# The experts' biases as one float32r product over 128 rows

## The chip, the core and the metric

The kernel runs on one core of a Trainium2 chip. The metric is device time in microseconds (us), the median over runs of the whole program. A profile is one execution recorded by the hardware profiler; its busy times and waits belong to that execution. The engines are named as in the profile: PE is the matrix engine (PEld its weight loads), DVE the vector engine, ACT the scalar engine, POOL the GpSimd engine, and SP the engine that here only issues transfers. Each takes its instructions in program order, and waits on semaphores for the others.

## The reference, cut to what matters

Four residual stages follow each other on 2048 tokens of width 256: cross attention, a mixture of eight experts, a windowed attention over a context of 1601 rows, and a slot layer. The change touches the second:

```python
logits  = einsum('bsd,ed->bse', layernorm(x), router_w) + router_b
probs   = softmax(logits)
weights = max(probs);  top1 = argmax(probs)
y_all   = einsum('bsd,eod->bseo', layernorm(x), expert_w) + expert_b   # 8 experts
y       = take_along_axis(y_all, top1)        # the chosen expert's row
x       = x + y * weights
```

The kernel computes all eight products for each token and weights them with a gate: a row of eight numbers, zero except for the chosen expert, where it holds the weight. The biases then come in as `gate @ expert_b`, a product of a tokens x 8 matrix with an 8 x 256 matrix.

## The kernel before

**Stages.** The attention (lines 720 to 909) takes the first 800 us. Everything after it stands in one part of the program (from line 912), with new pools in the memory that the attention leaves, so its loads cannot start before the attention is over. First come 13 loads on SP's queue (lines 929 to 945: the context, `W_aT`, `W_cT`, the slot layer's weights, about 5 MB) and 13 small ones on POOL's queue (lines 946 to 965). SP's loads are given out over eight semaphores in turn; a load whose semaphore still belongs to an earlier transfer waits, in SP's order, until that one has landed.

**Blocks.** The tokens are cut into five blocks (`BLOCKS`, line 967): three of four tiles of 128 tokens, and two of two tiles. `experts(lb)` (line 1031) walks one block: for every tile, four pairs of experts, each an fp32 product into a PSUM buffer `y_ps` (four of these exist, pool `ps_y`), followed by two DVE instructions that multiply with the gate and add to `x_sb` (line 1048). A `yield` ends each pair. After each second tile the biases are added: two fp32 matmuls with the turned gate as weights, `gT` (8 x 128), and the biases `eb` (8 x 256) as the moving side (line 1059), and one DVE addition (line 1061).

**The turned gate.** `turned_gate` (line 1010) runs once per block, after the first tile: it transposes the gate, 128 x 8 per tile, into a PSUM bank (pool `ps`, three banks, function `bank`) and copies it on ACT to `gT`, 8 x 512. `eb` was loaded with the experts' weights (line 144), at 203 us in the profile.

**What runs beside.** Between two pairs, `aside(3)` (line 1391) advances up to three other generators by one step each: `front` of the next block (layer norm, transposes, routing), `window` (a preparation for the third stage, once), `slots` (a preparation for the fourth, once), and, for blocks already through the experts, `windowed` followed by `weights`. The order of these steps is the program order of each engine; the scheduling of this part is by hand. When the blocks are through, the remaining generators run alone, with filler matmuls (`busy`), and the slot layer ends the program.

**Names for the steps of the prediction.** Line 107 is the normalizing DVE instruction of the layer norm, line 102 its POOL instruction (`ln_rstd`), line 1001 the transposes that wait for it; lines 1072 to 1136 are DVE's part of `window`; line 1115 its first instruction in the second step. Line 1233 is the ACT tanh into `th` and line 1235 the POOL addition that reads it; `th` has two buffers. Line 1312 is a large POOL addition in `weights`, line 1351 the DVE product `alpha`. Line 1369 is a subtraction on 64 partitions that makes a second part of a float32r number, and line 1523 a float32r product of 128 rows by 256 columns in the slot layer's end.

## Time and profile before

| | us |
|---|---|
| median of three runs (1083.15, 1085.77, 1083.15) | 1083.15 |
| the profiled execution | 1085.9 |
| its span | 1084.1 |
| PE busy, matmuls | 961.7 (89%) |
| DVE busy | 749.3 (69%) |
| ACT busy | 516.9 (48%) |
| POOL busy | 71.9 (7%) |
| last attention matmul ends, loads of the second part start | 800.5 |
| block 0 of the experts, first and last pair | 800.4 to 859 |
| last expert pair of the last block | about 1013 |

The profile's page gives busy time by engine, then the span in 40 slices, then the queues, then the chain of work that ended last, followed back from the last instruction to what released each step, then the costliest groups of instructions. Further views answer questions on one engine in one stretch: its instructions in order of time, with the idle time before each and what ended it. An fp32 matmul stands in the records as two instructions, a float32r matmul as one. Busy shares are averages over stages with different limits; for a change in one stage, what counts is which engine is waited for there.

### The profile page before, as it was taken

What the parts mean: (1) busy time and instruction counts of PE and PEld (TensorE: products, weight loads), DVE (VectorE), ACT (ScalarE), POOL (GpSimd) and SP (SyncE); (2) the same over time, 40 slices, a digit from 0 to 9 for tenths busy, and PEclk for the clock granted to TensorE, in tenths of its full rate; (3) what the DMA queues carried; (4) which work ended last, traced back from release to release, by engine and by line L of the source; (5) the groups of instructions that cost most, each with busy time, mean ns of one, the idle gap of its engine ahead of it and who ended that gap; (6) DMA issues with size and microseconds to landing.
All of it is one profiled execution on the core that took longest, in us unless ns stands there. A gap on an engine that the chain in (4) does not pass through costs nothing.

```text
span 1084.1 us, 14756 instructions
## 1 busy us (share of the span) xinstructions
PE 961.7 (89%) x5742; PEld 448.1 (41%) x5742; DVE 749.3 (69%) x1415; ACT 516.9 (48%) x614; POOL 71.9 (7%) x96
## 2 busy tenths in 40 slices
PE   6787888989989899898889989899997999999986
PEld 2234333444443343343334434344343455545543
DVE  6456867878777787878787876977016566675754
ACT  2423546666646565656566665665840011221331
POOL 4000200000010000001000000000020003021210
PEclk8777979999999999999999999998998999999999
DMA  4763721310102100001210110100033000000002
GB/s 157 162 150 93 145 71 44 107 27 3 28 2 71 60 13 28 16 13 28 88 29 2 28 28 2 28 2 1 2 108 116 1 1 0 1 1 1 1 0 78
DMA packets 32277, 46.96 MB, mean 43 GB/s; under 512 B 6412, under 2 KB 21269, under 8 KB 31951
## 3 DMA queue, kind: packets, MB, share of 16 engines
q1 hardware_dynamic: 30478, 43.65, 15.0%
q10 hardware_dynamic: 1232, 1.61, 0.4%
q8 instruction: 45, 0.74, 0.3%
q0 software_dynamic: 496, 0.76, 0.3%
q14 instruction: 26, 0.21, 0.1%
HBM read 26.77 MB, written 14.04 MB: 38 GB/s over the span
## 4 chain that ended last, share of the span: by engine, by line
PE 67%; DVE 24%; issue 4%; DMA 2%; ACT 1%; POOL 1%; SPq 0%; POOLq 0%; DVEq 0%; ACTq 0%
PE acc L849 18%; PE s_ps L883 14%; DVE mx L262 12%; PE a_ps L257 11%; PE y_ps L1041 7%; PE a_ps L240 2%; DVE xn L107 2%; DVE x_sb L1048 2%; PE a_ps L498 1%; PE a_ps L824 1%; PE o_ps L1227 1%; DVE ln_stats L96 1%; PE a_ps L284 1%; PE x_ps L461 1%; PE a_ps L461 1%
## 5 line engine op out<-in xcount | busy, mean ns | idle before, releaser
L262 DVE TENSOR_REDUCE mx<-a_ps 128x2 f32<-128x804 f32 (+1 forms) x645 | 494.2, 799 | 133.9 <-PE a_ps L257 123.4
L888 ACT ACTIVATE es<-s_ps 128x1024 f32<-128x1024 f32 (+1 forms) x416 | 405.6, 1021 | 231.8 <-PE s_ps L883 225.0
L257 PE MATMUL a_ps<-kb,qb 50*128 50x402 bf16 x992 | 235.3, 353 | 47.7 <-DVE mx L262 32.5
L883 PE MATMUL s_ps<-qt,kt 52*128 52x512 f32 (+1 forms) x832 | 242.4, 530 | 2.1 <-DMA qt<-nT 2.1
L849 PE MATMUL acc<-es,v 128*32 128x512 f32 (+1 forms) x1664 | 233.0, 632 | 0.0
L257 PEld LDWEIGHTS <-qb 50*128 50x128 bf16 x1024 | 81.2, 95 | 294.6 <-issue 276.3
L883 PE MATMUL s_ps<-ql,kt 52*128 52x512 f32 (+1 forms) x832 | 196.9, 403 | 0.0
L883 PEld LDWEIGHTS s_ps<-qt,kt 52*128 52x128 f32 (+1 forms) x832 | 102.9, 196 | 29.2 <-ACT es L888 16.1
L883 PEld LDWEIGHTS s_ps<-ql,kt 52*128 52x128 f32 (+1 forms) x832 | 108.5, 192 | 0.4
L1041 PE MATMUL y_ps<-expert_wT_sb,xT 128*128 128x512 f32 x192 | 89.8, 598 | 0.0
L102 POOL TENSOR_TENSOR ln_rstd<-ln_ve,mhalf 128x2 f32<-128x2 f32 (+2 forms) x28 | 21.1, 754 | 781.3 <-DVE ln_ve L100 780.0
L1048 DVE SCALAR_TENSOR_TENSOR x_sb<-y_ps,r_gate,x_sb 128x256 f32<-128x256 f32 x96 | 46.3, 482 | 32.5 <-PE y_ps L1041 30.7
L849 PEld LDWEIGHTS acc<-es,v 128*32 128x32 f32 (+1 forms) x1664 | 33.4, 109 | 54.5 <-issue 52.9
L1041 PEld LDWEIGHTS y_ps<-expert_wT_sb,xT 128*128 128x128 f32 x192 | 34.1, 191 | 31.9 <-issue 30.8
L1004 ACT COPY xT<-tr_ps 128x512 f32<-128x512 f32 (+1 forms) x28 | 13.4, 493 | 53.3 <-PE tr_ps L1001 53.3
L798 DVE RECIPROCAL rec<-a_ps 128x16 f32<-128x16 f32 x16 | 4.1, 258 | 49.4 <-PE a_ps L240 49.4
L107 DVE TENSOR_SCALAR xn<-x_sb,ln_mv,ln_rstd 128x256 f32<-128x256 f32 x64 | 32.8, 554 | 1.1 <-POOL ln_rstd L102 1.1
L1041 PE MATMUL y_ps<-expert_wT_sb,xnT 128*128 128x512 f32 x64 | 32.2, 631 | 0.0
L1001 PE MATMUL tr_ps<-ident,xn 128*128 128x128 f32 x88 | 17.6, 296 | 10.9 <-DVE xn L107 10.9
L284 PE MATMUL a_ps<-ident,nsp 128*8 128x128 f32 x64 | 10.0, 279 | 19.3 <-DVE nsp L275 18.9
L96 DVE BATCH_NORM_STATS2 ln_stats<-x_sb 128x6 f32<-128x256 f32 x64 | 23.3, 413 | 3.4 <-POOL x_sb L1235 3.4
L1048 DVE SCALAR_TENSOR_TENSOR x_sb<-y_ps,gate,x_sb 128x256 f32<-128x256 f32 x32 | 15.4, 483 | 13.6 <-PE y_ps L1041 13.0
(343 smaller groups left out, 727.9 us busy)
## 6 DMA issues: line engine op xcount, KB each, us to landing
qt<-q_rows SPq DMA_DIRECT2D x32, 192.0 KB
q_rows<-qhi SPq DMA_DIRECT2D x8, 512.0 KB
qb<-q_rows SPq DMA_DIRECT2D x30, 96.0 KB
kt<-expert_wT_sb SPq DMA_DIRECT2D x24, 100.5 KB
q_rows<-qp SPq DMA_DIRECT2D x8, 256.0 KB
q_rows<-qlo SPq DMA_DIRECT2D x8, 256.0 KB
ql<-q_rows SPq DMA_DIRECT2D x32, 64.0 KB
expert_wT_sb<-in_expert_wT SPq DMA_DIRECT2D x1, 2048.0 KB
```

Of the source, the lines that this page charges most:

```text
L96: nc.vector.bn_stats(stats[:rows, i, :], src[:, i, :])
L102: nc.gpsimd.tensor_tensor(rstd[:rows, :n], ve[:rows, :n], mhalf[:rows, :n], ALU.pow)
L107: nc.vector.tensor_scalar(dst[:, i, :], src[:, i, :], mv[:rows, i, 0:1], rstd[:rows, i : i + 1], ALU.subtract, ALU.mult,)
L240: nc.tensor.transpose(ps[:, t * P : (t + 1) * P], src[:, t, c * P : c * P + n], ident)
L257: nc.tensor.matmul(ps[:, k, :CH], qb[u % 2][rows, pl, t * P : (t + 1) * P], kb[g][rows, pl, c * CH : (c + 1) * CH], start=True, stop=True,)
L262: nc.vector.tensor_reduce(flat[:, n : self.n], ps[:, : self.n - n, :CH], AX.X, ALU.max)
L461: nc.tensor.matmul(ps[:n, :D], ctxT[:, c, i * P : i * P + n], wv[:, c, :], start=c == 0, stop=c == 1,)
L849: nc.tensor.matmul(acc[HP * j : HP * (j + 1), :], v[:n, i, h * VW : h * VW + HP], es[j // 2][:n, j % 2, :], start=i == 0, stop=i == NS - 1,)
L883: nc.tensor.matmul(ps[:n, h, :], kt[u % NG][rows, pl, i * P : i * P + n], q[u % nq][rows, pl, :], start=k == 0, stop=k == 1,)
L888: nc.scalar.activation(e[:n], ps[:n], AF.Exp)
L1041: nc.tensor.matmul(ps.rearrange("p e d -> p (e d)"), xT[:, c, tok], ew[:, c, pair * 2 * D : (pair + 1) * 2 * D], start=c == 0, stop=c == 1,)
L1048: nc.vector.scalar_tensor_tensor(xb[:, t, :], ps[:, k, :], gate[:, t, e : e + 1], xb[:, t, :], ALU.mult, ALU.add,)
```

## The change

The product with the biases gets 128 rows, in float32r, in place of 8 rows in fp32. The gate is repeated sixteen times side by side (128 x 128 per tile), so that its transpose has the gate in every group of eight rows. Of the transposed gate, rows 0 to 63 keep the first part (the value rounded to float32r) and rows 64 to 127 the second (what the rounding left). The bias tile is zero but for rows 0-7, 32-39, 64-71 and 96-103, which hold the biases; of these, groups 0 and 64 keep the first part and groups 32 and 96 the second. One product over 128 rows then sums all four combinations of parts.

- `bias_parts`, new, is a generator that runs beside block 0. Its first step clears the tile `eb4` on POOL and issues four loads of the biases on SP's queue; its second makes the parts on DVE, with one copy and two subtractions. The load of `eb` at line 144, and the tile, are gone.
- `turned_gate` becomes a generator of three steps, advanced after each of the first pairs of a block's first tile: a POOL copy that repeats the gate (128 x 512 for four tiles), the transposes and the ACT copy (now 128 partitions), and a DVE subtraction on the upper 64 partitions that reads the PSUM bank again.
- `th` has one buffer in place of two.

```diff
-    eb = keep.tile([NE, D], F32, name="eb")
...
-        nc.sync.dma_start(eb, a["expert_b"])
...
+    def bias_parts():
+        eb4 = moe.tile([P, 2, D], F32, name="o", bufs=3)[:, 0, :]
+        nc.gpsimd.memset(eb4, 0.0)
+        for k in range(4):
+            nc.sync.dma_start(eb4[k * 32 : k * 32 + NE, :], a["expert_b"])
+        yield
+        parts = late.tile([P, D], F32R, name="eb_parts")
+        nc.vector.tensor_copy(parts, eb4)
+        for k in (1, 3):
+            rows = slice(k * 32, (k + 1) * 32)
+            nc.vector.tensor_tensor(
+                parts[rows], eb4[rows], parts[rows].bitcast(F32), ALU.subtract
+            )
+        eb_of["parts"] = parts
+        yield
 
     def turned_gate(lb):
         gate, nt = gate_of[lb], BLOCKS[lb][1]
-        ps = bank([NE, nt * P], "g_ps")
+        g16 = moe.tile([P, TPB, P // NE, NE], F32, name="g16", bufs=1)[:, :nt]
+        nc.gpsimd.tensor_copy(g16, gate.unsqueeze(2).to_broadcast([P, nt, P // NE, NE]))
+        yield
+        ps = bank([P, nt * P], "g_ps")
         for t in range(nt):
-            nc.tensor.transpose(ps[:, t * P : (t + 1) * P], gate[:, t, :], ident)
-        gT = moe.tile([NE, LB], F32, name="gT")
+            nc.tensor.transpose(
+                ps[:, t * P : (t + 1) * P], g16[:, t].rearrange("p k e -> p (k e)"), ident
+            )
+        gT = gT_of[lb] = moe.tile([P, LB], F32R, name="gT")
         nc.scalar.copy(gT[:, : nt * P], ps)
-        return gT
+        yield
+        nc.vector.tensor_tensor(
+            gT[NSLOT:, : nt * P], ps[NSLOT:], gT[NSLOT:, : nt * P].bitcast(F32), ALU.subtract
+        )
+        yield
...
+        gT = turned_gate(lb)
         for t in range(nt):
...
+                if t == 0:
+                    next(gT, None)
                 yield
-            if t == 0:
-                gT = turned_gate(lb)
             if t % 2:
...
-                    nc.tensor.matmul(ps[:, k, :], gT[:, tok], eb, start=True, stop=True)
+                    nc.tensor.matmul(
+                        ps[:, k, :], gT_of[lb][:, tok], eb_of["parts"], start=True, stop=True
+                    )
...
-            th = moe.tile([P, 2, D], F32, name="th")
+            th = moe.tile([P, 2, D], F32, name="th", bufs=1)
...
-    beside = [window()]
+    beside = [bias_parts(), window()]
```

In the instruction order that comes of it, SP's four new loads stand behind its 13 loads of the second part, and on four of the eight semaphores: those that last belonged to `w2`, `WhhT`, `WihT` and `wq`. On DVE the three instructions of `bias_parts` stand between the second layer-norm statistics of block 1 (line 100, at 815.9 us in the profile before) and line 1115. On POOL the gate's copy for block 0 stands ahead of the first `ln_rstd`, and the clearing of `eb4` ahead of the index instruction of `window` (line 1086). On PE the transposes for block 0 stand behind the attention's last output product (line 824), and two pairs of `y_ps` that ran ahead of them now follow them.

More of the change, by code (lines that the diff above doesn't have):

```diff
@@ L1005, in normed @@
             yield
-    turned_of, gate_of = {0: xnT}, {0: gate_0}
+    turned_of, gate_of, gT_of = {0: xnT}, {0: gate_0}, {}
+    eb_of = {}
+    def bias_parts():
[13 more added lines that the diff above has]
+        yield
     def turned_gate(lb):
         gate, nt = gate_of[lb], BLOCKS[lb][1]
-        ps = bank([NE, nt * P], "g_ps")
+        g16 = moe.tile([P, TPB, P // NE, NE], F32, name="g16", bufs=1)[:, :nt]
+        nc.gpsimd.tensor_copy(g16, gate.unsqueeze(2).to_broadcast([P, nt, P // NE, NE]))
+        yield
+        ps = bank([P, nt * P], "g_ps")
         for t in range(nt):
-            nc.tensor.transpose(ps[:, t * P : (t + 1) * P], gate[:, t, :], ident)
-        gT = moe.tile([NE, LB], F32, name="gT")
+            nc.tensor.transpose(
+                ps[:, t * P : (t + 1) * P], g16[:, t].rearrange("p k e -> p (k e)"), ident
+            )
+        gT = gT_of[lb] = moe.tile([P, LB], F32R, name="gT")
         nc.scalar.copy(gT[:, : nt * P], ps)
-        return gT
+        yield
[3 more added lines that the diff above has]
+        yield
     def front(lb):
@@ L1034, in experts @@
         xb, nt = of_block(lb)
-        gT = None
+        gT = turned_gate(lb)
         for t in range(nt):
```

## The prediction

> **What bounds the kernel now.** I read the page's chain of waits first, then PE's and DVE's instructions in order of time where the change lies, then SP's, then the table by stretches of time.

> ```profile
> PE 67%; DVE 24%; issue 4%; DMA 2%; ACT 1%; POOL 1%; SPq 0%; POOLq 0%; DVEq 0%; ACTq 0%
> ```

> PE sets the end for two thirds of the span, DVE for a quarter. The change lies behind 800 us. There the table by stretches (columns: stretch, length, busy PE, PEld, DVE, ACT, POOL with counts, granted clock, DMA share, GB/s) says where PE is full:

> ```profile
> 824.00:860.00 36.00, 36.00 (x121) 17.35 (x121) 15.75 (x42) 1.49 (x4) 0.00 (x0) 0.94 0.00 1
> 860.00:911.00 51.00, 49.39 (x184) 27.14 (x183) 33.35 (x104) 6.41 (x12) 6.87 (x9) 1.00 0.00 0
> 911.00:962.00 51.00, 47.74 (x175) 26.41 (x174) 35.81 (x107) 10.11 (x17) 8.35 (x8) 1.00 0.00 1
> 962.00:1004.00 42.00, 38.51 (x152) 22.23 (x151) 30.17 (x93) 10.09 (x19) 7.63 (x7) 1.00 0.00 0
> ```

> From 824 us on PE is busy all the time, then 92 to 97% of it: what PE saves there is saved, and a delay handed to PE at 824 is never made up. Before 824 it is otherwise. PE's lines, then DVE's:

> ```profile
> 814.41 1.88 PE L1041 MATMUL y_ps<-expert_wT_sb,xnT 128*128 128x512 f32 x4
> 820.02 0.65 PE L1001 MATMUL tr_ps<-ident,xn 128*128 128x128 f32 x2 [3.72 <-DVE xn L107]
> 823.33 0.80 PE L1001 MATMUL tr_ps<-ident,xn 128*128 128x128 f32 x2 [2.66 <-DVE xn L107]
> ...
> 815.90 0.17 DVE L100 TENSOR_SCALAR ln_ve<-ln_mv 128x2 f32<-128x2 f32 x1
> 817.08 0.22 DVE L1115 CAST posr<-posr_i 128x64 f32<-128x64 int32 x1 [1.01 <-POOL posr_i L1113]
> ...
> 822.86 0.73 DVE L107 TENSOR_SCALAR xn<-x_sb,ln_mv,ln_rstd 128x256 f32<-128x256 f32 x2
> ```

> PE stands idle for 3.72 and 2.66 us, each time for DVE's normalizing instruction (line 107), and DVE has hardly a gap from 817.08 to 824. So in this stretch DVE's order sets the end, and whatever is put between line 100 and line 1115 goes straight onto the path. The change puts three instructions there, the first of which waits for a transfer.

> **The wait for the biases (the largest term).** The four new loads stand behind SP's big ones. Its last, and the traffic (stretch table, same columns):

> ```profile
> 816.24 2.43 SPq L77 DMA_DIRECT2D wo_sb<-in_wo  x1
> 820.00:822.00 2.00, 0.65 (x2) 0.28 (x2) 1.66 (x11) 0.39 (x2) 0.00 (x0) 0.85 1.12 325
> 822.00:824.00 2.00, 0.68 (x3) 0.53 (x4) 1.95 (x6) 0.29 (x1) 0.00 (x0) 0.50 0.48 154
> ```

> SP is not through with its last issue until 816.24 + 2.43 = 818.67. The third and fourth loads then wait for the semaphores of `WihT` and `wq`. From the sizes, 83% of SP's bytes lie up to `WihT`; summing the GB/s of the 2 us stretches, and taking off POOL's 0.76 MB, they have passed at about 820.5. So the fourth load is issued at about 821.5. The traffic ends at about 823. I let the biases land at 823.5 to 824, say 823.8; ends: 822.7 (with the last big bytes) and 826 (if the four issues take 1 to 3 us as `wo`'s 2.43 did).

> [...]

> What DVE loses: from 817.08 to 823.8 is 6.7 us. The copy of 128x256 I take at 0.33 (a DVE instruction of that shape from memory, line 1300), the two subtractions at 0.42 each (line 1456's row): 1.2 us. The gate's subtraction, placed before the first line 107, is 0.69 (line 1369: 64x512, 694 ns). Sum: **+8.6 us** on DVE and so on PE's second transposes (823.33). POOL's copy of the gate (about 1 us) and the clearing (about 0.25) push line 1086 and then DVE by some 1.3 us before the wait, and PE's two moved pairs end near 819.6 in place of 816.3; both lie inside DVE's wait and cost nothing. If it were gone, the 1.3 us would count. PE's clock is granted at 0.50 between 822 and 824 already[...].

> **The saving on PE.** The product before and the float32r row of the same form as the new one (128 rows, 256 columns):

> ```profile
> 833.52 1.13 PE L1059 MATMUL eb_ps<-eb,gT 8*128 8x256 f32 x4
> 1071.98 3.78 PE L1523 MATMUL f_ps<-s,aT 128*128 128x256 f32 x24 [0.46 <-ACT s L1513]
> ```

> The four records of two fp32 matmuls take 1.06 us of PE's time on the chain. The first of the 24 float32r records stands alone for 0.46 us; the other 23 take 3.32 us, 0.144 each. So two take 0.3, and each of eight places saves 0.76. Seven lie where PE is nearly full; the last (1016 us) beside waits for ACT and POOL: **-5.3 us**.

> **What blocks 1 to 4 pay.** Transposes: the row with 128 columns of weights (line 1365) takes 0.59 per four on the chain, that with eight (line 1015) 0.53: +0.2 in all. ACT's copy has the same length per partition (574 against 586 ns for the slot layer's 128x512): nothing. The subtractions: 0.69, 0.69, 0.43, 0.43 on DVE. In block 1 DVE has slack (33 of 51 us). In blocks 2 and 3 DVE runs without gaps from 911.9 to 932 and PE waits 1.84 us for `alpha` (line 1351), so there they count: +1.1. POOL's copies come behind `ln_rstd` (POOL is idle from 906.2 to 914.15), so no `ln_rstd` waits; but in this trace line 107's pair takes 2.80 us beside POOL's line 1312 and 0.73 elsewhere, and a copy of about 1 us beginning at 906.2 meets line 107 at 906.25, with PE's transposes close behind. Ends: 0 and 1 each for two blocks; I take half: +1.0. A bank held one step longer, three of them: 0 to 1, I take 0.2. `th`: two tanh are 4.3 us apart (895.33, 899.64), and POOL's addition is done at 897.27; the single buffer costs nothing until that is 2.3 us later.

> **Sum.** +8.6 - 5.3 + 0.2 + 1.1 + 1.0 + 0.2 = **+5.8 us**, against the profiled execution's 1085.9 (span 1084.1): 1091.7. Two of the three runs lie 2.7 lower, at the median of 1083.15; from there it is 1089.0. Two terms (wait, POOL) I may have set high, so **1088.5**.

> **Rivals.**
> - *Hidden wait* (not slower). The small loads slip in between the big ones and land by 818, or DVE reaches them later than I think. For it: they are 32 KB together[...]. Against: SP itself is busy until 818.67. Then +8.6 falls to about +1.9 and the sum is -0.9; with no POOL collisions and no bank wait -2: 1081 to 1082. It decides once the biases land before 819. A gain of over 0.3% (3.2 us) needs all eight savings as well.
> - *The wait is longer.* [...]they land at 826: +2.2, 1091; with collisions at their upper end, 1092.
> - *No gain on PE.* Weight loads of 128 rows bound the float32r product: the PEld rows of line 1523 are 186 ns where those of line 1059 were 184, so little speaks for it. Then the whole -5.3 is missing: 1094.

> **How the numbers follow.** Changes of under 0.3% (1079.9 to 1086.4) can't be told from none. Forecast 0.58, longer wait 0.17, no gain 0.05, hidden wait 0.20. My forecast's own range is 1085 to 1091; of it a tenth falls below 1086.4. Hidden wait divides between same and faster. So: slower 0.74, same 0.17, faster 0.09. Range 1083 to 1093.

> **What would show it.** In the changed profile: DVE idle before its first `eb_parts` instruction, about 6 us, released by a transfer, ending near 823.8; PE's second idle time before line 1001's transposes longer by 8 us; two bias records in 0.3 us where four took 1.06; between block 0's end and the end of the experts a gain of some 3 us. I am wrong if DVE doesn't wait at `eb_parts`, or if PE makes up the delay by 860 us.

## The result, and the profile after

| | before | after |
|---|---|---|
| median of 7 runs each, us | 1084.42 | 1095.55 |
| range of the runs, us | 1079.99 to 1088.06 | 1091.60 to 1098.20 |
| profiled span, us | 1084.1 | 1093.7 |
| PE busy, us | 961.7 | 956.2 |
| DVE busy, us | 749.3 | 753.7 |

The ratio of the times is **1.0103, interval 1.0074 to 1.0132**: slower by some 11 us, of which the two profiled executions show 9.6. The direction was as predicted; the time lies outside the range, and the loss is about twice the 5.8 us of the sum.

Busy times say little: PE does 5.5 us less and the kernel takes 10 us more. First the chain of waits of the page after, shares of the span by engine:

```profile
PE 64%; DVE 26%; issue 4%; DMA 3%; ACT 1%; POOL 0%; SPq 0%; POOLq 0%; DVEq 0%; ACTq 0%
```

PE's share fell by three points and DVE's and the transfers' rose. Where that is, the order of time shows: SP's issues, then DVE's instructions (start, length, engine, line, what; in brackets the idle time before and what ended it).

```profile
815.74 1.46 SPq L77 DMA_DIRECT2D wo_sb<-in_wo  x1
817.31 4.59 SPq L1016 DMA_DIRECT2D o<-in_expert_b  x4
```
```profile
817.84 0.17 DVE L100 TENSOR_SCALAR ln_ve<-ln_mv 128x2 f32<-128x2 f32 x1
824.53 0.30 DVE L1019 CAST eb_parts<-o 128x256 fp32r<-128x256 f32 x1 [6.53 <-DMA o<-in_expert_b]
824.86 0.85 DVE L1022 TENSOR_TENSOR eb_parts<-o,eb_parts 32x256 fp32r<-32x256 f32 x2
```

The bracket is the predicted wait: DVE is through with the statistics at 818.0 and stands for 6.53 us, until the fourth of the four small loads, whose issue ended at 821.90, has landed. An issue itself takes 0.27 to 0.31 us; 3.3 of the 4.59 us are waits of the second and third issue for semaphores that still belong to earlier loads, 1.1 for `WhhT` and 2.2 for `WihT`. The chain of waits shows the end of it: the load of `wq`, and when it has landed the fourth load of the biases, 2.78 us from issue to landing (start, length):

```profile
808.95 12.67 DMA wq_sb<-in_wq
821.63 2.78 DMA o<-in_expert_b
```

PE pays with DVE, at the same two transposes that waited 3.72 and 2.66 us before; then the new product:

```profile
829.47 0.80 PE L999 MATMUL tr_ps<-ident,xn 128*128 128x128 f32 x2 [9.20 <-DVE xn L107]
832.89 0.80 PE L999 MATMUL tr_ps<-ident,xn 128*128 128x128 f32 x2 [2.63 <-DVE xn L107]
...
842.57 0.80 PE L1086 MATMUL eb_ps<-eb_parts,gT 128*128 128x256 f32 x2
```

The second transposes moved from 823.33 to 832.89. The product stands as two records where four stood.

**How later times are compared.** The attention, whose instructions are the same in all these kernels but for the early loads of the biases, ends at another time in each profiled execution: the first pair of block 0 begins between 797.83 and 804.58 us. So each time is counted from that first pair (800.40 before, 800.12 after), and the difference to before is taken of that. By this measure the second transposes are 9.84 us late, and the first float32r product of the slot layer's end (1071.98 before, 1081.68 after) is 9.98 us late. Between these two points lie all savings and the costs of blocks 1 to 4, and they cancel: **of the 5.3 us that PE was to save, nothing net is left.** That, not the wait, is what the prediction missed most.

PE's lines show two reasons. In block 1, before and after:

```profile
890.35 0.62 PE L1218 MATMUL t_ps<-ident,sc 128*65 128x128 f32 x4 [0.77 <-DVE sc L1213]
```
```profile
900.40 0.62 PE L1247 MATMUL t_ps<-ident,sc 128*65 128x128 f32 x4 [1.79 <-DVE sc L1242]
```

These transposes of the third stage wait for DVE's softmax, and a bias product stands just ahead of them. It is shorter now, PE gets to the wait sooner than DVE does, and waits 1.02 us longer. (DVE is later too: the softmax comes 10.33 us behind the kernel before, 0.5 more than the second transposes.) The same in blocks 2 and 3: 1.35 us where 0.33 stood. The other reason is line 107, which now has the gate's subtraction ahead of it. PE waits for it 0.77 us in block 1 and, at places where it waited 0 and 0.26 us before, 1.31 and 1.06 us in blocks 2 and 3:

```profile
935.25 0.65 PE L999 MATMUL tr_ps<-ident,xn 128*128 128x128 f32 x2 [1.31 <-DVE xn L107]
```

### The profile page after: what moved, and what is told of

Its sections match the earlier page's. It is cut to its first block, busy times and chain, and to the rows that moved or that the text cites. A ratio compares the mean times of both kernels' runs of the same rounds, so it can differ in the third digit from the quotient of the medians.

```text
span 1093.7 us, 14741 instructions
## 1 busy us (share of the span) xinstructions
PE 956.2 (87%) x5726; PEld 445.4 (41%) x5726; DVE 753.7 (69%) x1423; ACT 517.2 (47%) x614; POOL 74.7 (7%) x102
## 3 DMA queue, kind: packets, MB, share of 16 engines
q10 hardware_dynamic: 1232, 1.61, 0.4%
## 4 chain that ended last, share of the span: by engine, by line
PE 64%; DVE 26%; issue 4%; DMA 3%; ACT 1%; POOL 0%; SPq 0%; POOLq 0%; DVEq 0%; ACTq 0%
PE acc L847 18%; PE s_ps L881 13%; DVE mx L260 12%; PE a_ps L255 11%; PE y_ps L1068 6%; DVE x_sb L1075 2%; DVE xn L107 2%; PE a_ps L238 2%; DVE ln_stats L96 2%; PE a_ps L496 1%; PE o_ps L1256 1%; DMA wq_sb<-in_wq 1%; PE a_ps L822 1%; PE a_ps L282 1%; PE x_ps L459 1%
## 5 line engine op out<-in xcount | busy, mean ns | idle before, releaser
L881 PE MATMUL s_ps<-qt,kt 52*128 52x512 f32 (+1 forms) x832 | 239.5, 524 | 2.4 <-DMA qt<-nT 2.4
L102 POOL TENSOR_TENSOR ln_rstd<-ln_ve,mhalf 128x2 f32<-128x2 f32 (+2 forms) x28 | 21.2, 757 | 746.4 <-DVE ln_ve L100 745.1
L107 DVE TENSOR_SCALAR xn<-x_sb,ln_mv,ln_rstd 128x256 f32<-128x256 f32 x64 | 33.3, 563 | 1.1 <-POOL ln_rstd L102 1.1
L999 PEld LDWEIGHTS tr_ps<-ident,xn 128*128 128x128 f32 x88 | 12.0, 149 | 34.1 <-DVE xn L107 20.9
```

What stands on the lines that cost most here:

```text
L102: nc.gpsimd.tensor_tensor(rstd[:rows, :n], ve[:rows, :n], mhalf[:rows, :n], ALU.pow)
L107: nc.vector.tensor_scalar(dst[:, i, :], src[:, i, :], mv[:rows, i, 0:1], rstd[:rows, i : i + 1], ALU.subtract, ALU.mult,)
L881: nc.tensor.matmul(ps[:n, h, :], kt[u % NG][rows, pl, i * P : i * P + n], q[u % nq][rows, pl, :], start=k == 0, stop=k == 1,)
L999: nc.tensor.transpose(ps[:, t * P : (t + 1) * P], xn[:, t, c * P : (c + 1) * P], ident)
```

## The experiments

Each run has its expectation ahead of it. Ratios are against the kernel before, which ran beside; times relative to the first pair are of one profiled execution.

| kernel | ratio (interval) | second transposes, us | slot layer's end, us |
|---|---|---|---|
| the change | 1.0103 (1.0074 to 1.0132) | +9.8 | +10.0 |
| e1 early loads | 1.0032 (1.0009 to 1.0055) | +3.6 | +5.1 |
| e2 parts five steps later | 1.0021 (1.0002 to 1.0040) | +3.5 | +3.5 |
| e8 loads on ACT's queue | 1.0087 (1.0063 to 1.0110) | +7.1 | +7.2 |
| e12 change, gate one tile later | 1.0064 (1.0041 to 1.0087) | +8.3 | +6.0 |
| e6 = e2, gate one tile later | 0.9991 (0.9973 to 1.0009) | +0.5 | -1.4 |
| e9 = e6 with fillers | **0.9948 (0.9931 to 0.9964)** | +0.7 | -3.3 |

**The wait (e1, e2).** e1 brings the loads back to where `eb` was loaded; e2 leaves them and only uses them later.

```diff
 # e1, beside the load of router_b
+        nc.gpsimd.memset(eb4, 0.0)
+        for k in range(4):
+            nc.sync.dma_start(eb4[k * 32 : k * 32 + NE, :], a["expert_b"])
 # e2, in bias_parts
-        yield
+        for _ in range(5):
+            yield
         parts = late.tile([P, D], F32R, name="eb_parts")
```

> The changed kernel, but the bias tile is cleared and loaded where the old load stood (with the experts' weights, at about 203 us); the three DVE instructions that make the parts stay where they are, the parts lie in an output tile to save room. Theory A (the transfer's wait is the loss): DVE's idle 6.5 us before the first eb_parts instruction is gone, PE's second transposes after the normalizing instruction come about 2.4 us later than in the kernel before instead of 9.6, and the whole is 1.5 to 3 us slower than before (ratio 1.0015 to 1.003). Rival B (the moved transposes, POOL's copy and its place ahead of the first ln_rstd delay block 0 whatever the loads do): the delay at the second transposes stays at 6 us or more and the ratio at 1.006 or more.

> The changed kernel with the loads as they are, and the making of the parts five steps (pairs of experts) after the loads instead of one. Theory A: DVE finds the biases landed (they landed at 824.5 us, DVE is there at about 830), no wait; PE's second transposes are some 2 us later than before (POOL's copy and clearing ahead of the index instruction 1.3, the gate's subtraction 0.7), the whole 0.5 to 2 us slower than before (ratio 1.0005 to 1.002). If the loads themselves cost (traffic, SP's semaphores), it stays 4 us or more slower. Against e1 it tells whether it matters where the transfer runs or only where it is waited for.

In both DVE no longer waits for the biases; in e2 the copy has no idle time in front of it:

```profile
831.99 0.28 DVE L1020 CAST eb_parts<-o 128x256 fp32r<-128x256 f32 x1
```

By the ratios 7 to 9 of the 11 us are gone (their intervals are 2 to 3 us wide to either side). So the wait is the larger part. But both stay slower than before and a little slower than expected, with their second transposes still 3.5 us late: something else in block 0 costs that much once the wait doesn't cover it.

**Whose queue (e8).** The same four loads at the same step, issued by ACT.

```diff
-            nc.sync.dma_start(eb4[k * 32 : k * 32 + NE, :], a["expert_b"])
+            nc.scalar.dma_start(eb4[k * 32 : k * 32 + NE, :], a["expert_b"])
```

> The changed kernel with its four loads of the biases issued from ACT instead of SP, at the same step. Theory A (the wait is the order of SP's queue, where they stand behind 5 MB): they land within about 2 to 3 us of POOL's clearing at 813.8, by 817; DVE's idle time before eb_parts falls from 6.5 to under 1 us; ratio near 1.002, as without the wait. Theory B (the traffic of the other loads delays them, whoever issues them): they land at 821 or later, DVE waits over 4 us, ratio 1.006 to 1.010.

ACT's issues, then DVE:

```profile
817.55 1.57 ACTq L1016 DMA_DIRECT2D o<-in_expert_b  x4
```
```profile
823.94 0.29 DVE L1019 CAST eb_parts<-o 128x256 fp32r<-128x256 f32 x1 [3.79 <-DMA o<-in_expert_b]
```

ACT could issue when POOL had cleared the tile, at 817.52 (the expectation's 813.8 was the start of POOL's copy, not of the clearing). Its four issues take 1.57 us against 4.59 on SP, yet from the end of the last (819.12) to the landing it is 4.8 us. Counted from the first pair, the biases are there at 21.7 us in place of 24.4. The time is theory B's, and the wait, 3.79 us, falls just short of its 4: leaving SP's queue gains 2.7 us, not the whole wait. What remains is put down to the traffic of the other loads (323 to 347 GB/s from 816 to 822, 200 from 822 to 824), but this run is no clean test of it. SP's own timing changed too: between the issues of `WhhT` and `WihT` SP now stands for 6.0 us (0.07 in the change), and its last big load is issued by 21.2 us behind the first pair, where it was 17.1 in the change.

From the end of the last issue to the landing it is 2.6 us on SP (821.90 to about 824.5), whose fourth load went out when the traffic was ending (313 GB/s from 820 to 822, 96 from 822 to 824, none later), and 4.8 on ACT, with 347, 330 and 200 GB/s beside it. On a queue of their own the loads did not land sooner behind their issue.

**What is left in block 0 (e7, e6).** The turned gate's steps run beside the first tile in the change. In block 0 this puts all of the two moved pairs behind the attention's output products, where they no longer fill PE. e7 does only that to the kernel before; e6 takes it back from e2.

```diff
 # e7, in the kernel before
-            if t == 0:
-                gT = turned_gate(lb)
+                if t == 0 and pair == 1:
+                    gT = turned_gate(lb)
 # e6, in e2
-                if t == 0:
+                if t == 1:
                     next(gT, None)
```

> The kernel before with its gate turned two pairs earlier, so that block 0's two pairs of y_ps come behind the attention's output products as in the change; product, biases and all else as before. Theory A: PE idle for some 2 us before the second product of line 824, which takes about 3.4 us instead of 2 at a clock of 0.5; second transposes 1 to 2.5 us later; ratio 1.001 to 1.0025. Theory B (the moved pairs cost nothing, as predicted): ratio 0.9995 to 1.0005.

> The version with the parts five steps later (ratio 1.0021), with the turned gate's steps beside the second tile instead of the first and nothing else. Theory A: block 0's order of PE is that of before, the second product of line 822 takes 2 us, second transposes at most 1 us later than before (3.5 without this edit), and the ratio falls to 0.999 to 1.0005. Theory B (the order is worth nothing, DVE's subtraction and POOL's copy are the rest): the ratio stays at 1.0015 to 1.0025, with second transposes over 2 us late.

PE in e7, the two halves of the output product; the second took 1.99 us before:

```profile
806.57 1.99 PE L824 MATMUL a_ps<-WoT_sb,aT 128*128 128x256 f32 x8 [0.68 <-ACT aT L815]
810.73 3.31 PE L824 MATMUL a_ps<-WoT_sb,aT 128*128 128x256 f32 x8 [2.17 <-DVE x_sb L829]
```

The table of stretches of the changed kernel has the reason (columns: stretch, length, busy PE, PEld, DVE, ACT, POOL with counts, granted clock, DMA share, GB/s):

```profile
808.00:810.00 2.00, 0.00 (x0) 0.00 (x0) 1.39 (x7) 0.00 (x0) 1.41 (x4) 1.00 0.97 266
810.00:812.00 2.00, 1.93 (x5) 1.60 (x6) 0.01 (x1) 0.00 (x0) 1.08 (x2) 0.61 1.02 214
812.00:814.00 2.00, 1.54 (x4) 0.67 (x2) 0.42 (x1) 0.00 (x0) 0.25 (x2) 0.54 1.20 208
```

PE does nothing for 2 us, the granted clock goes from 1.00 to 0.61 and 0.54, and the same eight products take 3.47 us. In the kernel before, half of a moved pair (807.96, 1.02 us) lies in this gap, the wait is 1.45 us and the clock stays at 1.00:

```profile
810.00:812.00 2.00, 1.57 (x7) 1.42 (x8) 0.37 (x1) 0.00 (x0) 1.16 (x3) 1.00 1.04 210
```

The moved pairs alone made e7's second transposes 1.2 us later, its end 0.4 us, and its ratio 1.0024 (1.0006 to 1.0042); the profile's 0.4 us lies just under the interval's lower end of 0.7. In e6 the second product takes 1.99 us again, and the second transposes are 3.0 us earlier than in e2. The moved pairs are 1.2 of these; the other 1.8 are the rest of what stood ahead of the path in this order, POOL's copy of the gate (0.61 us) ahead of line 102 and DVE's subtraction (0.69 us) ahead of line 107 among it. These come to 1.3; they were not separated, and 0.5 us have no name.

**Wait and order together (e12).** The change with only the gate's steps moved as in e6, the wait left in.

> The changed kernel with its parts and their wait where they are, and only the turned gate's steps beside the second tile instead of the first. Theory A (the order of the two pairs lies inside the wait for the biases): DVE still waits till about 24 us after block 0's first pair, the wait is longer by what the order gave back (6.5 to about 8 us), second transposes earlier by 0.7 us at most for the gate's subtraction; ratio 1.008 to 1.010. Theory B (wait and order add up): ratio 1.007 or less, 3 us under the changed kernel.

```profile
825.23 0.29 DVE L1019 CAST eb_parts<-o 128x256 fp32r<-128x256 f32 x1 [7.80 <-DMA o<-in_expert_b]
...
829.43 0.71 PE L999 MATMUL tr_ps<-ident,xn 128*128 128x128 f32 x2 [12.48 <-DVE xn L107]
```

At the second transposes theory A is near: the wait grows from 6.53 to 7.80, and they come 1.6 us earlier, 0.7 of it the subtraction and 0.6 an earlier landing in this execution. But the end comes 4.0 us earlier, and the ratio is nearer theory B's (its interval reaches into A's). By the third `l_ps` (line 1353) e12 is even 5.6 us earlier; it then loses 1.6 by a fall of the clock in the last gap, below, that the change doesn't have. So 4.1 us come out of the blocks behind the second transposes. Pieces of under 1 us are the most of it, such as PE's shorter waits for line 107 (0.31 and 0.46 us where the change has 0.77 and 1.31). The largest single piece, 1.7 us, is the change's clock, which falls once more in block 1:

```profile
890.00:892.00 2.00, 2.00 (x20) 2.00 (x20) 1.22 (x5) 0.00 (x0) 0.00 (x0) 1.00 0.00 0
892.00:894.00 2.00, 2.00 (x12) 2.00 (x12) 0.12 (x2) 0.23 (x1) 0.00 (x0) 0.59 0.00 0
894.00:896.00 2.00, 2.00 (x3) 0.80 (x3) 1.22 (x3) 0.42 (x1) 0.00 (x0) 0.56 0.01 4
```

This fall, with PE full, is in e2 too (0.54 from 886 to 888), and in e4, where four `y_ps` records take 3.42 us in place of 1.88. It is not in e1 and e8, which have the same order here; these two have a fall in block 3 instead (3.58 and 3.44 us for four such records), at 1.6 to 1.7 us. So each of the five profiles with the change's order has one fall in blocks 1 to 3, and none of the nine others has. It is not shown that the order brings it; what the traces say of the cause stands behind the last gap.

**The product's saving alone (e3).** The kernel before with its 8 rows in float32r, and nothing else.

```diff
-        gT = moe.tile([NE, LB], F32, name="gT")
+        gT = moe.tile([NE, LB], F32R, name="gT")
+    ebr = moe.tile([P, 2, D], F32, name="o", bufs=3)[:NE, 0, :].bitcast(F32R)
+    nc.scalar.copy(ebr, eb)
```

> The kernel before, with the bias product in float32r over the same 8 rows: ACT writes the turned gate as float32r, ACT makes one float32r copy of the biases at the start of the second part. The second parts of gate and biases are left out, so the biases come in rounded. Nothing is added on DVE, POOL or SP. It prices PE's saving alone. The forecast's term: -5.3 us (ratio 0.995). Theory A (in blocks 1 to 4 PE reaches the next DVE wait that much earlier, only block 0's two places count): -1.8 to -2.5 us (ratio 0.9977 to 0.9983), with PE's waits for the window softmax (line 1213) and for line 107 longer by some 0.7 us a block.

Ratio 0.9996 (0.9982 to 1.0010), less than either expectation. Each place gains 0.63 us on PE. But the first place of blocks 1 and 2, and block 3's only one, stand ahead of the transposes that wait for the softmax, which wait just 0.63 us longer:

```profile
890.70 0.62 PE L1220 MATMUL t_ps<-ident,sc 128*65 128x128 f32 x4 [1.40 <-DVE sc L1215]
```

The last place (block 4) is lost in the same way at the wait for line 107 near 1022: 0.81 us in place of 0.18. So four of eight places can reach the end. There a second loss begins, in this run and several others: the fourth `h_ps` comes later than the longer wait explains.

**The last gap (e9, e10, e11).** Four more filler products behind the third `h_ps` (block 2) near 1019, in e6 (e9) and in e3 (e11); and the kernel before with four fewer ahead of it (e10).

```diff
-        busy(2)
+        busy(6 if lb == 2 else 2)
```

> The version with the parts five steps later and the gate one tile later (ratio 0.9991), with four more filler products on PE behind the third h_ps near 1019, where PE then waits some 2 us for line 107. Theory A (the eighth saving lets PE stand idle for 2 us there, the clock falls to 0.5 and takes some 2.1 us back): with the gap filled as before the change, the wait ahead of line 107 is 0.2 us again, the clock stays at 1.00, the fourth h_ps is not later by 2 us than the third; ratio 0.997 to 0.998. Theory B (the loss there has another cause, such as DVE and POOL): the fourth h_ps still loses 2 us against the third, ratio 0.999 or more.

> The kernel before with the first four filler products of its last stage left out, near 1017, so that PE comes 0.9 us earlier to its wait for line 107 near 1022; the product with the biases is that of before. The fillers compute nothing that is used. Theory A (a longer idle time of PE there can make its clock fall): the wait grows from 0.18 to about 1.1 us, and the time stays or grows, by up to 2.1 us in an execution in which the clock falls: ratio 1.000 to 1.002, never a gain. Theory B (PE earlier is the end earlier): the end comes 0.9 us earlier, ratio 0.999.

> The kernel before with the product in float32r over 8 rows (second parts left out; ratio 0.9996), and four more filler products behind the third h_ps. Theory A (the clock's fall in the last gap took 2.2 us of its saving): the fall stays away, five of eight savings of 0.63 us reach the end: span 3 us shorter relative to the attention's end, ratio 0.9975. Theory B: ratio 0.9996 as without the fillers.

PE and the stretches in e6:

```profile
1022.83 0.33 PE L999 MATMUL tr_ps<-ident,xn 128*128 128x128 f32 x1 [1.12 <-DVE xn L107]
1024.10 0.33 PE L999 MATMUL tr_ps<-ident,xn 128*128 128x128 f32 x1 [0.94 <-DVE xn L107]
...
1025.94 1.91 PE L972 MATMUL busy_ps<-xnT 128*128 128x512 bf16 x4
```
```profile
1024.00:1026.00 2.00, 1.90 (x10) 1.35 (x11) 1.83 (x11) 0.62 (x2) 0.00 (x0) 0.81 0.00 0
1026.00:1028.00 2.00, 2.00 (x6) 1.04 (x5) 1.53 (x7) 1.92 (x4) 0.00 (x0) 0.50 0.00 0
```

and in e9:

```profile
1017.50 0.33 PE L999 MATMUL tr_ps<-ident,xn 128*128 128x128 f32 x1 [0.22 <-DVE xn L107]
...
1020.28 1.06 PE L972 MATMUL busy_ps<-xnT 128*128 128x512 bf16 x4
```

In e6 PE waits 2.06 us with one transpose between, then runs at 0.81 and 0.50, and four fillers take 1.91 us in place of 1.06. In e9 the first wait is 0.22 and the clock stays at 1.00. From the third `l_ps` to the fourth `h_ps` it is 4.8 to 5.1 us in the four profiles where the first wait is at most 0.22 (before, e7, e9, e11). In the ten others it is 0.81 to 1.14: in four (the change, e2, e8, e10) the clock stays and the stretch takes 5.95 to 6.04 us, in six (e1, e3, e4, e5, e6, e12) the clock falls and it takes 7.2 to 7.7. So a gap of 2 us allows the fall and doesn't force it.

**What a fall follows.** The clock's record says more. In the profiles of before and of the change the granted clock is either 1.00 or 0.50 (a stretch's 0.61 or 0.81 is a mean over a change), and every stretch of one clock but the last is a whole number of 3.41 us steps long, 1 to 74 of them; the six falls of the last gap last 3.40 to 3.44 us each by their stretches of 2 us. A step begins 0.51 us behind the first pair before and 0.07 in the change; the falls behind 800 us last 1 to 4 steps, or till the end. To see what the step ahead of a fall holds, each PE record was priced by its columns: 0.83 ns a column in fp32, since records of 512 columns follow each other at 0.43 us, and about half of that in float32r and bf16 (records of 256 columns follow each other at 0.12 us on line 1523, of 512 at 0.22 on the fillers). This is an estimate, made when the runs were done. From 800 us on the two profiles have six falls; ahead of them the step holds 0 to 1.26 us of such work. The 153 steps at full clock with no fall behind them hold 1.30 us or more. In block 1 of the change PE is busy for all of the step, but with products of 8 and 65 columns for most of it, and the price is 1.26; in its last gap, where the clock stays, it is 1.30. So by this reading neither the gap's length nor a busy PE decides, but how few columns fall into one such step. It rests on these two profiles, the fall near the end of e11 (1.61 ahead of it) does not fit, and no run tested it. What is measured of gaps: 2.06 us in e6, with a transpose between, and 2.17 and 2.23 us without work in e7 and the change brought a fall; 1.99 us in e10 and 2.08 in the last gap of the change, with a transpose between, did not.

In e10 (0.9999, 0.9980 to 1.0018) the wait grew to 1.05 us, the clock held, and the end stayed where it was: time that PE saves there is worth nothing.

e9 is faster than both kernels, by more than expected. Of its 5.6 us (interval 3.9 to 7.5) its profile shows 3.3 behind the first pair. The rest lies ahead of it: the first pair came at 797.83, 2.6 us earlier than in the profile of before, and whether the attention is shorter in this program or was in this execution is open. e11 left its expectation: its profile's end is 3.1 us earlier behind the first pair, but its ratio is 0.9994 (0.9979 to 1.0009). Its profiled execution had the latest first pair of all, 804.58, and the same question is open there.

**The gate's second part on POOL (e4, e5).** `turned_gate` makes both parts on POOL ahead of the transposes (`hi` is the gate rounded to float32r, `half` the shape of eight repeats) and drops DVE's subtraction: e4 is e2 with that; e5 also has the gate one tile later, and `window` ahead of the biases.

```diff
-        nc.gpsimd.tensor_copy(g16, gate.unsqueeze(2).to_broadcast([P, nt, P // NE, NE]))
+        nc.gpsimd.tensor_copy(hi, gate)
+        nc.gpsimd.tensor_copy(g16[:, :, : P // NE // 2], gate.unsqueeze(2).to_broadcast(half))
+        nc.gpsimd.tensor_tensor(
+            g16[:, :, P // NE // 2 :], gate.unsqueeze(2).to_broadcast(half),
+            hi.bitcast(F32).unsqueeze(2).to_broadcast(half), ALU.subtract,
+        )
...
-        nc.vector.tensor_tensor(
-            gT[NSLOT:, : nt * P], ps[NSLOT:], gT[NSLOT:, : nt * P].bitcast(F32), ALU.subtract
-        )
```

> As e2, and the gate's second part is made on POOL before the transposes (round, copy, subtract on 128 partitions) instead of on DVE after them; DVE's five subtractions are gone. If these subtractions are what eats PE's saving in blocks 1 to 4, it is 1.5 to 2.5 us faster than e2; if PE's saving lies in stretches where PE waits for DVE anyway, the gain is under 1 us. POOL's longer work in block 0 (about 0.7 us more ahead of the index instruction) may take 0.7 of it.

> The changed kernel with three edits: the parts of the biases are made five steps later, the gate's second part is made on POOL ahead of the transposes (no DVE subtraction), and the turned gate's steps run beside a block's second tile instead of its first, with the step that clears the bias tile behind the first of window. Theory A (what is left of the loss without the wait is the order of the two pairs of y_ps in block 0, which lets PE stand idle and its clock drop): the second output product of line 822 takes 2 us again, not 3.46; second transposes within 0.5 us of before; the time 1 to 3 us under before, ratio 0.997 to 0.999, if the loss of about 2.3 us near 1030 stays away, otherwise 0.999 to 1.001. Theory B (the order costs nothing; the rest is POOL's copies): as the version with the order of the change and the same other edits, ratio 1.0007.

Ratios 1.0007 (0.9991 to 1.0024) and 1.0004 (0.9990 to 1.0019), both with the fall in the last gap. e4's second transposes are 0.4 us earlier than e2's, and its ratio is 1.5 us better, but the intervals overlap. Against e6's 0.9991 e5 shows no difference, so moving the subtraction to POOL is not shown to help once the gate comes a tile later.

## Why the prediction was wrong in size

By its own steps:

- **The wait: right, 1.2 us short.** 8.6 was forecast for the second transposes, 9.84 came, and by the path that was forecast: SP's issues stood for the semaphores of the big loads up to `wq`, and the fourth went out at 821.63 (forecast 821.5). The landing was put at 823.8 and is at about 824.5 (24.4 us behind the first pair, where 823.8 meant 23.4). The parts took 1.15 us (1.2 forecast), the gate's subtraction 0.69. That the cover of 1.3 us from POOL would count once the wait was gone was right, and the rival of the hidden wait should have had it in its sum; with the subtraction that made 2.0, and 3.5 us came out.
- **The saving of 5.3 us: the step that failed.** "What PE saves there is saved" does not follow from a PE that is 92 to 97% busy. The size of a place was even too small. Four `y_ps` records alone take 1.72 us to the next start; with the product behind them it is 2.92 to 2.95 before and 2.01 to 2.04 after. So two float32r records add 0.3 us, as forecast, but the four in fp32 added 1.2 and not 1.06: 0.91 us at five of the eight places (waits and the clock blur the others), 0.63 with 8 rows in e3, 0.76 forecast. But the nearly full PE still has its few waits for DVE, just behind four of the eight products. What became of the saving shows in the delay against before, from place to place:

| place | delay, us |
|---|---|
| second transposes | 9.84 |
| block 0's second product | 8.32 |
| softmax transposes beside block 1 | 10.33 |
| routing product of block 3 | 9.07 |
| softmax transposes beside block 2 | 10.37 |
| routing product of block 4 | 9.14 |
| softmax transposes beside block 3 | 9.93 |
| third `l_ps` | 9.01 |
| fourth `h_ps` | 9.97 |

PE gains 4.9 us in four stretches and gives 5.1 back in four.

- **Where it was given back.** Of the 2.0 us in block 1, 1.7 are the clock's fall, for which the prediction had no term there. The 1.3 and 0.8 in blocks 2 and 3 come with the waits for line 107 of 1.31 and 1.06. The forecast had the subtractions count in these blocks, but at `alpha`, where PE's wait stayed (1.84 and 1.85 us); and "in block 1 DVE has slack" failed, with 0.77 us of wait. The last 1.0 is the last gap, where PE's first wait grows from 0.18 to 1.14:

```profile
1033.04 0.33 PE L999 MATMUL tr_ps<-ident,xn 128*128 128x128 f32 x1 [1.14 <-DVE xn L107]
```

- **Saving and costs of blocks 1 to 4 together.** Forecast were -5.3 and +2.5, so -2.8; +0.14 came, 2.9 us more. How this divides was not measured. If the four places of e3 count at 0.91 us each, the saving is 3.6 in place of 5.3 and the costs are 3.8 in place of 2.5; that is an estimate. POOL's copy took 0.62 us at most, not 1, and line 107's pair beside it 0.99 and 0.78 us in place of 0.73. The single `th` buffer cost nothing that a trace shows.
- **The moved pairs "cost nothing": right only under the wait.** Bare, they are 1.2 of the 3.0 us between e2 and e6, by way of a clock that the prediction saw fall near 822 and didn't look for near 810.
- **The rivals.** The longer wait (landing at 826) and no gain on PE (1094) were both named; what came lies above both, at 1095.55, and the second was nearest in effect, for another reason than weight loads.
- **A size taken off by feel.** The sum gave 1089.0 from the median of runs shown and was rounded down to 1088.5, though no term had been shown too high.

So the 9.98 us of the profile lie 4.2 over the sum of 5.8: 1.2 by the wait and 2.9 by the saving and the blocks behind it. The medians of the runs differ by 11.1; one profile of each can't place the rest. That the direction came out right owes nothing to the saving: the wait alone was larger than all that PE could have saved.

## What to carry to other kernels

A busy share of 95% doesn't say that a saving counts: look for the next wait of that engine behind each place, and ask whether what it waits for also comes earlier; where it doesn't, the saving ends there. The load that was moved to where it is used stood behind 5 MB of others here, and DVE waited 6.53 us for it; with the load where it was (e1), or its first use five steps later (e2), it did not wait. When an order is changed, look at the gaps it opens on PE as well as at what it delays, since the clock behind a gap of 2 us took another 1.1 to 1.7 us here. With four filler products in such a gap e9 stands at 0.9948, without them e6 at 0.9991.
